# First chunk's replicas on TensorE instead of through DRAM, and later constants off VectorE, in a selective-scan kernel

## The chip, the cores and the metric

The kernel runs on one core of a Trainium2 chip, in one launch. The metric is the device time of an execution in microseconds, the median of three runs. Everything is float32. The core has five engines with a queue each: TensorE (PE, with its weight loads PEld), VectorE (DVE), ScalarE (ACT), GpSimd (POOL) and SyncE (SP), which issues nearly all DMAs here. Every engine works through its own instructions in the order in which the program emits them.

## The reference

The input x is 4 x 128 x 128 x 128. Layer 0 is a selective state-space layer along the 16,384 positions of each image; layer 1 is a Fourier-domain filter. The change lies almost wholly in layer 0, whose core is:

```python
u = silu(conv1d(x_in) + conv_b)                 # 256 channels
dt, Bm, Cm = split(u @ x_proj_w.T)              # 8, 16, 16
delta = softplus(dt @ dt_proj_w.T + dt_proj_b)
A = -exp(A_log)                                 # 256 x 16
h = h * exp(delta * A) + delta * Bm * u         # per position, state 256 x 16
y = sum(h * Cm) + u * D
```

After it come a gate with silu(z), an output projection, a group norm, silu and a residual. Layer 1 takes a group norm, a 1x1 product with `agg_w`, a pooled softmax over four filters, and a filter applied in the frequency domain.

## The kernel before

Layer 0 is cut into 128 chunks of 512 positions (32 chunks for each of 4 images). The 256 channels are two halves `j`; a half is 4 groups of 32 channels (`DG`). The 16 states are 4 sets of 4 (`SQ`). A work item for a scan is a 128x512 tile: 32 channels times 4 states on the partitions, 512 positions along the free dimension. A chunk has 8 **units**, (j, r), of 4 such tiles each, p = 0 to 3, and 16 **slots** (`NP`): a slot handles two tiles of a unit. Slots are the clock of a hand-written order: every step of the program has a slot number and a phase within the slot, all steps are sorted by these, and instructions are emitted in that order. Steps that prepare chunk k (`pre(k)`) start up to 14 slots ahead of their own chunk's count.

For a tile four things are needed:

- `da` = exp(delta * A): ScalarE, line L409, from `rdelta`, a copy of 32 channels' delta on 4 x 32 partitions (a *replica*).
- the input term. For p = 0 it comes as `b`, from TensorE: du = delta * u is transposed (`du_turn`, L306), scaled by each of 4 states' B and written as `bt` (`bt_act`, L318, 16 instructions a chunk on ScalarE), and transposed back (`dbu_turn`, L399). For p = 1 to 3 GpSimd multiplies `rdu`, the replica of du, with `rB` (`dbu`, L379) into `hb`.
- the scan itself, on VectorE (L428), four 128x512 scans a unit.
- the product with `rC`: on VectorE for p = 2, 3 (L430) and on GpSimd for p = 0, 1 (L435); TensorE then sums over states into `y` (L449). ScalarE keeps the last state of every scan (L431 and L575).

Ahead of that, chunk k goes through `load`, `h1` (L207, L212), `xm` (L217, L225), the convolution as 8 products (L242), silu (L247), `xd` (L258, L262), dt (L281), delta by Softplus (L287), and z (L231, L236, its Silu at L250). `xd` holds B and C as well: it is written to DRAM (`bc`, L266) and read back by `bc_load` (L274) with every row spread over 32 partitions. The replicas go the same way: delta and du are written to DRAM (`dd`, L289 and L325) and read back by `rep_load` (L333), four DMAs of 256 KB for each of delta and du and each half j. du itself is a GpSimd product (`du_pool`, L324). ScalarE reloads its function table (1.28 us each) when it changes between Exp, Silu and Softplus.

For chunk 0 nothing runs ahead of it to cover this preparation. There `rep_load` and `bc_load` are issued in an order of their own on SP: replica of delta, B, replica of du, C. TensorE does chunk 1's `h1` and `xm` between the two `du_turn` of chunk 0.

`first_constants` loads the weights and prepares some of them on VectorE (`wck`, L102; `amat`, L104 and L105; `diag`, L108). `later_constants` loads what later stages need, and `later_products` (L136 to L146), emitted after the scans of slot 33 (chunk 2), prepares these on VectorE: `fwm` negated, `eps`, `ones`, `weff0` from two products, and `bias0` from a TensorE product.

PSUM tiles come from small pools: `pp` (two banks), `pt`, `y`, and one bank each for `b0`, `da1`, `da2`, `da3`; a tile waits until the bank's former reader is done. Layer 1 follows after the last chunk and is not touched.

## Time and profile before

| | |
|---|---|
| median of 3 runs | 7065.94 us (7059.47 to 7074.77) |
| profiled execution | 7065.28 us |
| its span | 7063.4 us |
| VectorE busy | 6838.7 us (97%) |
| GpSimd busy | 6806.9 us (96%) |
| ScalarE busy | 6167.3 us (87%) |
| TensorE busy | 5631.0 us (80%) |
| granted TensorE clock, mean | 0.93 |

Times in the profile count from the start of the span. A timeline line gives start, duration, engine, source line, operation, out <- in, shapes, the number of instructions merged (x), and in brackets how long the engine was idle before and what ended that. A waits line gives who waited for whom, total us, times, longest. Names without numbers stand for all chunks' tiles; PEq and SPq are the sequencers of TensorE and SyncE.

### The profile page before, as it was taken

The page shows a single profiled execution, that of the slowest core. Times are in us where ns is not written, and L with a number is a line of the kernel's source. Part 1 is how long each engine was busy: PE and PEld are TensorE (multiplying, and loading weights), DVE is VectorE, ACT ScalarE, POOL GpSimd, SP SyncE. Part 2 cuts the span into 40 slices and gives each one's busy share as a digit, 9 for nine tenths or more (in the row PEclk, how much of TensorE's full clock was granted, in tenths as well). Part 3 has the DMA queues.
Part 4 walks back from the last instruction along what each step waited for, and adds up shares of the span by engine and source line. Part 5 has one row for each costly group of instructions (what it writes and reads, how often), then busy time and mean ns, then how long its engine had stood idle before and what let it go on. Part 6 is the DMA issues. An engine that isn't in the chain of part 4 may idle for free. (4 is left out here: it accounts for less than half of the span.)

```text
span 7063.4 us, 95476 instructions
## 1 busy us (share of the span) xinstructions
PE 5631.0 (80%) x28724; PEld 2681.6 (38%) x28724; DVE 6838.7 (97%) x7901; ACT 6167.3 (87%) x13836; POOL 6806.9 (96%) x3010
## 2 busy tenths in 40 slices
PE   7777777777777778887777788888777787878999
PEld 3333333333333333333333333333333333337888
DVE  7999999999999999999999999999999999998877
ACT  7888888888989888889999988889999988888886
POOL 7999999999999999999999999999999999997887
PEclk8899999999989989999999999999999999989999
DMA  6766766666778777777878777777877877777865
GB/s 152 164 161 150 164 158 153 161 156 165 194 183 194 182 168 174 179 179 171 201 190 196 196 170 175 178 179 170 201 191 192 200 173 175 173 174 273 272 221 192
DMA packets 759512, 1288.53 MB, mean 182 GB/s; under 512 B 81728, under 2 KB 192848, under 8 KB 758992
## 3 DMA queue, kind: packets, MB, share of 16 engines
q1 hardware_dynamic: 758704, 1281.90, 73.1%
q8 instruction: 226, 3.70, 0.2%
q14 instruction: 294, 2.41, 0.1%
q10 hardware_dynamic: 288, 0.52, 0.0%
HBM read 1025.52 MB, written 256.58 MB: 182 GB/s over the span
## 5 line engine op out<-in xcount | busy, mean ns | idle before, releaser
L379 POOL TENSOR_TENSOR hb<-rdu,rB 128x1536 f32<-128x1536 f32 (+2 forms) x1536 | 3613.1, 2370 | 38.5 <-DMA rdu<-dd 25.4
L409 ACT ACTIVATE da<-rdelta,amat 128x512 f32<-128x512 f32 x4096 | 2805.3, 704 | 105.6 <-DVE h L428 100.4
L435 POOL TENSOR_TENSOR hb<-h,rC 128x1024 f32<-128x1024 f32 (+1 forms) x1048 | 2410.3, 2301 | 75.1 <-DVE h L428 62.5
L428 DVE TENSOR_TENSOR_SCAN da<-da,st,hb 128x512 f32<-128x512 f32 x2000 | 2445.9, 1265 | 34.8 <-ACT da L409 34.1
L430 DVE TENSOR_TENSOR hb<-da,rC 128x512 f32<-128x512 f32 x2064 | 1307.8, 672 | 2.2
L428 DVE TENSOR_TENSOR_SCAN h<-da,st,b 128x512 f32<-128x512 f32 x992 | 1256.5, 1267 | 4.3 <-PE b L399 4.3
L449 PE MATMUL y<-hb,sel 128*32 128x512 f32 x8192 | 1242.8, 680 | 14.8 <-POOL hb L435 13.9
L428 DVE TENSOR_TENSOR_SCAN h<-da,st,hb 128x512 f32<-128x512 f32 x976 | 1221.5, 1253 | 2.6 <-ACT da L409 1.5
L399 PE MATMUL b<-ident,bt 128*128 128x128 f32 x4096 | 714.1, 295 | 492.9 <-DVE h L428 427.1
L242 PE MATMUL pp_cv<-xm,wck 128*128 128x512 f32 x2048 | 989.3, 627 | 2.9 <-ACT zs L236 1.6
L318 ACT ACTIVATE bt<-pt_dut,xdt 128x256 f32<-128x256 f32 x2048 | 851.0, 484 | 138.4 <-PE pt_dut L306 137.8
L399 PEld LDWEIGHTS b<-ident,bt 128*128 128x128 f32 x4096 | 517.1, 149 | 951.8 <-DVE h L428 704.3
L431 ACT COPY st<-da 128x1 f32<-128x1 f32 x2064 | 287.5, 163 | 446.1 <-DVE hb L430 442.3
L242 PEld LDWEIGHTS pp_cv<-xm,wck 128*128 128x128 f32 x2048 | 387.0, 199 | 633.5 <-issue 453.1
L306 PE MATMUL pt_dut<-ident,du 128*128 128x128 f32 x1024 | 198.3, 327 | 482.4 <-POOL du L324 451.5
L871 POOL TENSOR_TENSOR wb<-wb,term 128x1040 f32<-128x1040 f32 x166 | 398.9, 2403 | 50.2 <-ACT term L861 44.4
L445 PE MATMUL y<-u,diag 128*128 128x512 f32 x512 | 313.7, 697 | 163.5 <-DVE zs L459 163.0
L306 PEld LDWEIGHTS pt_dut<-ident,du 128*128 128x128 f32 x1024 | 140.8, 164 | 660.4 <-POOL du L324 590.5
L409 ACT ACT_TABLE_LOAD x262 | 336.1, 1283 | 4.6
L324 POOL TENSOR_TENSOR du<-delta,u 128x1024 f32<-128x1024 f32 x128 | 301.4, 2354 | 24.9 <-ACT delta L287 24.9
L449 PEld LDWEIGHTS y<-hb,sel 128*32 128x32 f32 x8192 | 170.4, 113 | 384.2 <-issue 244.5
L281 PE MATMUL pp_dt<-xd,wdt 128*128 128x256 f32 x1024 | 286.6, 404 | 25.9 <-ACT xd L262 8.9
(167 smaller groups left out, 8337.5 us busy)
## 6 DMA issues: line engine op xcount, KB each, us to landing
rdelta<-dd SPq DMA_DIRECT2D x1024, 256.0 KB, 4.9
rdu<-dd SPq DMA_DIRECT2D x1024, 256.0 KB, 7.8
rC<-bc SPq DMA_DIRECT2D x512, 256.0 KB, 7.1
rB<-bc SPq DMA_DIRECT2D x512, 192.0 KB, 4.4
dd<-delta SPq DMA_DIRECT2D x256, 256.0 KB, 7.6
dd<-du SPq DMA_DIRECT2D x128, 512.0 KB, 6.7
ft<-in_filt_w SPq DMA_DIRECT2D x108, 520.0 KB, 6.5
xr<-in_x SPq DMA_DIRECT2D x128, 256.0 KB, 3.0
```

The lines of the kernel that those rows point to most:

```text
L242: nc.tensor.matmul(ps["cv", j], w, d["xm"][:, t : t + T], start=t == 0, stop=t == KC - 1)
L306: nc.tensor.transpose(ps["dut"][:, 2 * t + j, :], d["du"][:, j, at : at + P], s.ident)
L318: nc.scalar.activation(d["bt"][:, 2 * h + t, :, q, :], src, AF.Copy, scale=d["xdt"][:, 2 * h + t, R + q : R + q + 1])
L379: nc.gpsimd.tensor_tensor(hb[:, p : p + n, :], d["du", j][:, m : m + n, :], d["B"][:, p - 1 : p - 1 + n, :], ALU.mult)
L399: nc.tensor.transpose(b[:, t * P : (t + 1) * P], src, s.ident)
L409: nc.scalar.activation(da, d["delta", j][:, m, :], AF.Exp, scale=s.amat[:, c : c + 1])
L428: nc.vector.tensor_tensor_scan(o, das[q], b, init, ALU.mult, ALU.add)
L430: nc.vector.tensor_tensor(hb[:, p + q, :], das[q], d["C"][:, p + q, :], ALU.mult)
L435: nc.gpsimd.tensor_tensor(hb[:, ps, :], h[:, q, :], d["C"][:, ps, :], ALU.mult)
L445: nc.tensor.matmul(y, s.diag[:, j, :], d["u"][:, j, :], start=True, stop=False)
L449: nc.tensor.matmul(y[m * DG : (m + 1) * DG, :], s.sel, d["hb", j, r][:, p, :], start=False, stop=r == NG - 1)
L871: nc.gpsimd.tensor_tensor(wb, wb, u[n].terms[f], ALU.add)
```

## The change

All of it concerns the preparation of chunk 0, that of chunk 1, and the constants.

- **Replicas of chunk 0, half j = 0.** `rep_mm` multiplies delta (or du) by `rep`, a 128 x 4 x 128 matrix made of copies of the identity's columns, so that TensorE writes 32 channels onto 4 x 32 partitions of a PSUM bank; `rep_copy` moves each of 8 such banks to SBUF, two on VectorE and six on ScalarE. The first half of chunk 0 no longer goes through `dd`; the second half does as before.
- **du of chunk 0** is made on VectorE in two products (`first_du`).
- **The 16 scaled pieces `bt` of chunk 0** are shared: ScalarE makes the 8 of du's first half of positions, VectorE the 8 of the second, from two PSUM banks (`pt` and `y`).
- **B and C of chunk 0** are loaded first on SP, ahead of the `dd` writes and the replicas.
- **Function tables**: a 1-element activation (`table`) of Softplus, and later of Exp, is put ahead of the first use.
- **Chunk 1's preparation**: load, `h1` and `xm` move ahead in the order (into banks `da1` to `da3`), most other steps move one slot back.
- **GpSimd's first product** of chunk 0 is split in one of 512 and one of 1024 columns.
- **Constants**: `eps` and `ones` are set at the start; `amat` is computed after chunk 0's `h1`; `later_products` goes from slot 33 to slot 39 and does `bias0`, `fwm` and the first product of `weff0` on ScalarE, moves that product to PSUM with an identity product on TensorE, and adds the second on VectorE.

```diff
     def first_constants(s):
+        s.eps = cpool.tile([P, 1], F32, tag="eps", name="eps")
+        nc.vector.memset(s.eps, EPS)
+        s.ones = cpool.tile([P, P], F32, tag="ones", name="ones")
+        nc.vector.memset(s.ones, 1.0)
...
-        nc.scalar.activation(amat, amat, AF.Exp)
-        nc.vector.tensor_scalar_mul(amat, amat, -1.0)
+        rep = s.rep = s.spare.tile([P, ND, P], F32, tag="o", name="rep", bufs=3)
+        for m in range(SQ):
+            nc.vector.tensor_copy(rep[:, :, m * DG : (m + 1) * DG], s.ident.rearrange("p (g d) -> p g d", d=DG))
...
+    def decay_rates(s):
+        nc.scalar.activation(s.amat, s.amat, AF.Exp)
+        nc.vector.tensor_scalar_mul(s.amat, s.amat, -1.0)
...
     def later_products(s, psum):
-        nc.vector.tensor_scalar_mul(s.fwm, s.fwm, -1.0)
-        nc.vector.memset(s.eps, EPS)
-        nc.vector.memset(s.ones, 1.0)
-        weff0 = s.weff0 = cpool.tile([P, C], F32, tag="weff0", name="weff0")
-        nc.vector.tensor_scalar_mul(weff0, s.wagg[:, 0, :], s.gam[:, 0:1])
-        nc.vector.scalar_tensor_tensor(weff0, s.wagg[:, 1, :], s.gam[:, 1:2], weff0, ALU.mult, ALU.add)
...
-        nc.vector.tensor_add(s.bias0, pb0[:, 0:1], s.bagg)
+        nc.scalar.activation(s.bias0, pb0[:, 0:1], AF.Identity, bias=s.bagg)
+        nc.scalar.mul(s.fwm, s.fwm, -1.0)
+        weff0 = s.weff0 = cpool.tile([P, C], F32, tag="weff0", name="weff0")
+        nc.scalar.activation(weff0, s.wagg[:, 1, :], AF.Copy, scale=s.gam[:, 1:2])
+        pw0 = psum("weff0")
+        nc.tensor.matmul(pw0[:, 0:C], s.ident, weff0, start=True, stop=True)
+        nc.vector.scalar_tensor_tensor(weff0, s.wagg[:, 0, :], s.gam[:, 0:1], pw0[:, 0:C], ALU.mult, ALU.add)
...
             def bt_act(h, n0, n1):
...
+                    if k == 0 and h:
+                        nc.vector.tensor_scalar_mul(o, src, scale)
+                    else:
+                        nc.scalar.activation(o, src, AF.Copy, scale=scale)
...
+            def first_du():
+                du = d["du"] = pq.tile([P, NH, T], F32, tag="du", name=f"du_{k}")
+                for j in range(NH):
+                    nc.vector.tensor_mul(du[:, j, :], d["delta"][:, j, :], d["u"][:, j, :])
+                nc.sync.dma_start(out=d["dd"][1, P:, :], in_=du[:, 1, :])
+            def table(f):
+                t = tiny.tile([P, 1], F32, tag="table", name=f"table_{f}")
+                nc.scalar.activation(t, s.ones[:, 0:1], f)
+            def rep_mm(tag, m, to):
+                ps[tag, m] = to(f"rep_{tag}_{m}")
+                nc.tensor.matmul(ps[tag, m], s.rep[:, m, :], d[tag][:, 0, :], start=True, stop=True)
+            def rep_copy(tag, m, copy):
+                if (tag, 0) not in d:
+                    d[tag, 0] = p2.tile([P, ND, T], F32, tag=f"r{tag}", name=f"r{tag}_{k}_0")
+                copy(d[tag, 0][:, m, :], ps[tag, m])
...
+            if k == 0:
+                return [
+                    (-14, "pe", load), (-7, "pe", h1_mm), (-6, "act", h1_act), (-5, "pe", xm_mm), (-4, "act", xm_act),
+                    (0, "pe", partial(cv_mm, 0)), (1, "pe", partial(cv_mm, 1)), (2, "act", silu_act),
+                    (3, "pe", xd_mm), (4, "act", xd_act), (4, "act", partial(table, AF.Softplus)), (5, "pe", dt_mm),
+                    (5, "pe", xd_turn), (5, "act", bc_load), (6, "act", dt_act), (6, "act", xd_turn_act),
+                    (6, "act", partial(table, AF.Exp)), (6, "dve", first_du),
+                    (7, "pe", partial(du_turn, 1)), (7, "pe", partial(du_turn, 0)),
+                    (8, "pe", partial(rep_mm, "delta", 0, psum)), (8, "pe", partial(rep_mm, "delta", 1, psum)),
+                    (8, "pe", partial(rep_mm, "du", 1, partial(bank, "da2"))),
+                    (8, "pe", partial(rep_mm, "du", 2, partial(bank, "da3"))),
+                    (8, "act", partial(bt_act, 0, 0, 8)), (8, "dve", partial(bt_act, 1, 0, 8)),
+                    (8, "dve", partial(rep_copy, "delta", 0, dve)), (8, "dve", partial(rep_copy, "delta", 1, dve)),
+                    (14, "act", partial(rep_copy, "du", 1, act)), (14, "act", partial(rep_copy, "du", 2, act)),
+                    (15, "pe", partial(rep_mm, "du", 3, psum)), (15, "act", partial(rep_copy, "du", 3, act)),
+                    (15, "pe", partial(rep_mm, "delta", 2, psum)), (15, "act", partial(rep_copy, "delta", 2, act)),
+                    (15, "pe", partial(rep_mm, "delta", 3, turn_bank)), (15, "act", partial(rep_copy, "delta", 3, act)),
+                    (15, "pe", partial(rep_mm, "du", 0, y_bank)), (16, "act", partial(rep_copy, "du", 0, act)),
+                    (10, "pe", partial(rep_load, 1)),
+                    (NP, "pe", z_mm), (NP, "act", z_act), (NP + 3, "act", z_silu),
+                ]
+            late = k == 1
...
+                (-14 - 10 * late, "pe", load), (-7 - 13 * late, "pe", h1_mm), (-6 - 13 * late, "act", h1_act),
+                (-5 - 6 * late, "pe", xm_mm), (-4 - 6 * late, "act", xm_act),
+                (late, "pe", partial(cv_mm, 0)), (1, "pe", partial(cv_mm, 1)), (2 + late, "act", silu_act),
...
-                n = min(NG - p, ND - m)
+                n = min(NG - p, ND - m) if u or p > 1 else 1
...
+        todo[-NP - 5, "act"].insert(0, partial(s.decay_rates, s))
-        todo[2 * NP + 1, "end"].append(partial(s.later_products, s, psum))
+        todo[2 * NP + 7, "end"].append(partial(s.later_products, s, psum))
...
-            todo[n - 1, "exps"].append(partial(exps, n, (1,) if n % 2 == 0 else (0, 1)))
+            todo[n - 1 - (n == 0), "exps"].append(partial(exps, n, (1,) if n % 2 == 0 else (0, 1)))
...
-                todo[n - 2, "dbu"].append(partial(dbu, n // 2))
+                todo[n - 2 + (n == 0), "dbu"].append(partial(dbu, n // 2))
```

## The prediction

> **What bounds the kernel now.** I first read the windows (busy time of each engine by stage, first numbers: length, then PE, PEld, DVE, ACT, POOL).
>
> ```profile
> 20.00:40.00 20.00, 11.92 (x39) 5.58 (x37) 0.00 (x0) 13.35 (x29) 2.34 (x1) 0.88 0.61 156
> 40.00:60.00 20.00, 15.20 (x43) 5.88 (x43) 12.51 (x13) 11.60 (x20) 14.76 (x6) 0.78 1.07 221
> 80.00:100.00 20.00, 17.35 (x76) 6.93 (x75) 20.00 (x22) 16.77 (x42) 20.00 (x9) 1.00 0.78 162
> 140.00:180.00 40.00, 31.60 (x120) 13.49 (x121) 39.41 (x43) 29.17 (x62) 35.43 (x15) 0.79 0.58 134
> ```
>
> From about 50 us on VectorE and GpSimd are both full, and VectorE stays so (499.8 of 500 us in the window 500 to 1000). So a microsecond at the start, or of VectorE work later, goes to the end almost whole, if GpSimd can follow. Only the first 50 us and one spot near 150 us are open to this change. Second, the waits of the first 100 us:
>
> ```profile
> DVE h L428 <- PE b L399: 30.1, 1, 30.1
> POOL hb L379 <- DMA rdu<-dd: 17.6, 1, 17.6
> DVE h L428 <- POOL hb L379: 6.9, 1, 6.9
> ```
>
> VectorE waits for the transposed pieces `b`, then for GpSimd's first product, which waits for the DRAM replica of du. Third, the timeline of the start, which dates these events, and VectorE's near 150 us:
>
> ```profile
> 24.70 0.92 SPq L289 DMA_DIRECT2D dd<-delta  x2
> 25.33 2.34 POOL L324 TENSOR_TENSOR du<-delta,u 128x1024 f32<-128x1024 f32 x1 [24.89 <-ACT delta L287]
> 28.48 1.94 ACT L318 ACTIVATE bt<-pt_dut,xdt 128x256 f32<-128x256 f32 x5 [3.04 <-PE pt_dut L306]
> 38.34 1.73 SPq L333 DMA_DIRECT2D rdu<-dd  x4
> 45.24 6.82 POOL L379 TENSOR_TENSOR hb<-rdu,rB 128x1536 f32<-128x1536 f32 x2 [17.57 <-DMA rdu<-dd]
> 48.71 1.22 DVE L428 TENSOR_TENSOR_SCAN h<-da,hb 128x512 f32<-128x512 f32 x1 [6.86 <-POOL hb L379]
> 53.26 1.21 DVE L428 TENSOR_TENSOR_SCAN h<-da,b 128x512 f32<-128x512 f32 x1
> ...
> 149.92 4.22 DVE L136 TENSOR_SCALAR fwm<-fwm 128x130 f32<-128x130 f32 x1
> 155.29 0.16 DVE L146 TENSOR_TENSOR bias<-pp_bias,agg_b 128x1 f32<-128x1 f32 x1 [0.55 <-PE pp_bias L145]
> 155.37 1.27 DVE L428 TENSOR_TENSOR_SCAN h<-da,st,b 128x512 f32<-128x512 f32 x1
> ```
>
> My marks are: VectorE begins unit 1 at 53.26, GpSimd ends its first two units at 52.06 (45.24 + 6.82), and the constants hold VectorE from 149.92 to 155.37, 5.45 us.
>
> **The change part by part.** Times are from the span's start; each is worked out from before's rows.
>
> *Front end.* TensorE now runs chunk 1's two h1 products before chunk 0's convolution. Their input is issued on SP at 8.86 (its place in SP's queue is unchanged) and the fastest landing of such a tile is 2.6 us, so 11.5; four passes at 0.45 us end at 13.2. The convolution began at 12.45, so +0.75 us; what queues behind the wait is the convolution and all of chunk 0. Moving `amat`'s Exp behind the Relus saves nothing here: xm is ready at about 10.5 and waits for the load. Then as before: 7.1 us of convolution, silu, xd, so xd ends at 22.2 (before 21.44).
>
> *Tables.* The Softplus table (1.28 us) was loaded at 22.69, when the dt product was ready. The 1-element dummy puts it beside that product: 22.2 to 23.5, dummy 0.25, delta 23.75 to 25.05 (two of 0.64). Before it ended at 25.26. The Exp table load moves too, from 37.32 to 25.35, with no change of count on ScalarE's path: table and dummy 1.55, xm of chunk 1 0.9, so ScalarE is free at 27.8.
>
> *du on VectorE.* GpSimd took 2.34 us (25.33 to 27.67). Two 128x512 products at 0.66 (rows L430 0.67, L459 0.66) overlap the second delta: end 25.8. Both transposes of du (0.66 each) end at 27.15 without waiting for a bank.
>
> *Scaled pieces.* ScalarE's 16 were spread to 40.06 by the second transpose and chunk 1's steps. Now ScalarE does 8 at 0.39 (5 in 1.94): 27.8 to 30.9. VectorE's 8 from PSUM are in no row: nearest are 0.28 (TENSOR_SCALAR 128x128) and 0.42 (COPY 128x256 from PSUM), far end 0.66 (128x512 product). I take 0.40, the same size: 26.5 to 29.7; at 0.66 it would end at 31.8 and cost about 2.
>
> *Replicas.* TensorE copies: eight 128x512 products, two passes each, 0.9 at 0.45 a pass (0.43 to 0.45 in the convolution), 1.77 at the slow 0.885 seen from 28.22. At 0.9 the first four end at 30.75. VectorE evicts delta 0 and 1 at 0.65 (between 0.55 for 128x384 and 0.66): 30.35 and 31.0. ScalarE: two Exp (0.69) to 32.3, du 1, 2, 3 at 0.535 (`zs`: two in 1.07) to 32.85, 33.4, 33.9, delta 2 and 3 to 35.0, three Exp to 37.05, du 0 to 37.6. Gone from SP's queue ahead of `rC`: eight replica issues of 256 KB, and half of each `dd` write; `rB` is issued at about 24.2, lands by 31.2 (7.0 us, the median there), `rC` by about 36: neither ends a wait, but were they late by more than 1.7 and 2.5 us they would.
>
> *First units.* GpSimd: 1.26 from 32.9, 2.35 to 36.5, then 3.43 from 37.65: 41.1, against 52.06: 10.9 earlier. VectorE: the third scan starts at 36.5 and unit 1 3.41 later (49.85 to 53.26 before): 39.9, 13.3 earlier. GpSimd no longer has a lead: 41.1 against the scan that needs it at 41.1; before 52.06 against 54.39.
>
> *What is late next.* ScalarE, in order. Silu's and Exp's table loads (2.57), z's Silu (1.06) and u's (1.25) now lie later relative to the scans, because chunk 1's steps are one slot later and the last-state copies before them wait for VectorE's products. I count unit 2's third scan waiting 1.8 us for its Exp, and unit 4's 0.6 behind Softplus. VectorE's 13.3 becomes 10.9, the same as GpSimd's. Bounds: nothing lost (13.3), or twice that (8.5).
>
> *Later constants.* Six VectorE instructions and a wait, 5.45 us, leave. One stays: 0.35, from PSUM. It waits for the last-state copy 0.16, bias 0.3, fwm and weff0 on ScalarE at 0.42 (row L676, 128x128), TensorE 0.35: 1.65 after the last product. That is 2.0 in place of 5.45, a saving of 3.4; VectorE's whole queue is behind it. If ScalarE and TensorE are ahead, 5.1; if ScalarE is late by the width of Exp pairs, 1.3 less. GpSimd can take the gain: it waited 3.85 us at 157.89 for just this. The 4.22 ends with GpSimd's instructions (150.47 + 3.57 = 154.04), while a TENSOR_SCALAR of the same width next to no GpSimd work took 0.16 at 154.20. eps and ones move to VectorE's idle start (0.23 us, idle until 7.95); the rep copies (four at about 0.2) and diag end at 10.6, before xm is needed at 13.2. Chunk 2 onward has the same instruction order on every engine except here.
>
> [...]
>
> [...] In the trace, TensorE's granted clock was 0.50 in 41 to 45 us after an idle of 2.40, and a pass took 0.89. After an idle of 1.82 (9.69) a pass took 0.50. [...]
>
> **Sum.** 10.9 + 3.4 = 14.3. The profiled execution took 7065.28 (span 7063.4 and 1.9 around it), 0.7 below the median 7065.94. 7065.3 - 14.3 = **7051 us**.
>
> **The rivals.**
> 1. *More gets through.* ScalarE is not late and the weff0 wait is hidden: 13.3 + 5.1 = 18.4, 7047. For it: my two waits assume that every copy in ScalarE's queue waits to the end; before's same place cost only 0.25 and 0.27. Against: GpSimd's own lead of 10.9.
> 2. *The start feeds late.* The replicas run at half clock (3.5 more), or VectorE's pieces at 0.66 (2), or the xt of chunk 1 lands after 8.2 us, the slowest seen (5.6). One or two of these: gain 6 to 10, 7055 to 7059. For it: the slow passes at 28.22; against: TensorE is busier than then.
> 3. *The start is hidden.* Something else than VectorE and GpSimd paces chunks 1 and 2 (chunk 1's softplus, `dd` write and replicas are one slot later), and only the constants count: 3.4, 7062. Against: no wait of VectorE on DMA in that range; before had 17 us from du's end (74.1) to its use (91.51), after the same.
> 4. *Slower.* Tiles moved in SBUF (eps, ones, the dummy) or a shifted phase of ScalarE against VectorE make each later chunk dearer. It needs 14.3 us over some 126 chunks to eat the gain, and 28.4, 0.23 us a chunk, to be slower by 0.2%. ScalarE's Exp waits at chunk turns are the place. At 0.28 a chunk: 7086. Against: same order; VectorE idles under 0.2 us in 500. From 2500 to 3000 it idles 8.7, so there is something to disturb.
>
> **How the numbers follow.** 0.2%, what a measurement tells from no change here, is 14.1 us: below 7051.8 is faster, over 7080.1 slower. Forecast 0.48 (7048 to 7055), rival 1 0.22, rival 2 0.17, rival 3 0.05, rival 4 0.08. Of the forecast I put 0.34 on the faster side, as both its waits are counted at their worst. Faster 0.34 + 0.22 = 0.56, slower 0.08, same 0.36. The range leaves rival 4 and half of rival 3 above: to 7063. Below, rival 1 with the median's own scatter (runs differ by 6 to 9): 7040.
>
> **What would show it.** First GpSimd product at 32 to 34 us; VectorE's scans without a long gap from about 36; unit 1 at 39 to 41; a wait of VectorE on ScalarE's Exp of 1 to 2 us near 48; delta's end near 25; convolution start near 13.2; replica products at 0.9; no 4 us instruction on VectorE near 137 to 145, and under 2 us of wait for pp_weff. I am wrong if xt lands late, if GpSimd starts after 37, or if later windows of 500 us take more than before.

## The result, and the profile after

The changed kernel took 7042.62 us (median of 9 runs, 7031.45 to 7049.56) beside 7065.94 for the kernel before (9 runs, 7049.93 to 7074.77): a ratio of 0.997, 95% interval 0.9961 to 0.9979. The profiled execution of the changed kernel took 7042.62 us, its span was 7040.8. Together with the runs beside the experiments, the kernel before has a mean of 7061.7 us (62 runs) and the changed one of 7042.9 (20 runs): 18.7 us less, give or take 3.0 (twice the standard error; single runs scatter by 6).

First the windows of the changed kernel, at the four stretches that were shown of before (length, then PE, PEld, DVE, ACT, POOL):

```profile
20.00:40.00 20.00, 18.52 (x65) 9.53 (x65) 12.08 (x19) 17.93 (x38) 6.63 (x3) 1.00 0.67 159
40.00:60.00 20.00, 13.89 (x70) 6.48 (x68) 18.41 (x20) 16.88 (x29) 20.00 (x10) 0.95 0.74 161
80.00:100.00 20.00, 18.45 (x82) 7.98 (x83) 20.00 (x22) 15.71 (x32) 20.00 (x9) 1.00 0.72 144
140.00:180.00 40.00, 29.18 (x129) 12.47 (x127) 37.35 (x40) 34.73 (x78) 39.32 (x18) 0.87 0.55 133
```

From 20 to 40 us VectorE does 12.1 us of work where it did none; GpSimd is full from 40 us on, where it had 14.8 of 20. Near 150 us VectorE has lost some of its fill (37.4 of 40) while GpSimd has gained (39.3, was 35.4): the 3.85 us that GpSimd waited there are gone.

Second, the timeline of the changed kernel, start and later constants (start, duration, engine, line, operation; L488 and L490 are the scans and VectorE's products, L439 and L495 GpSimd's products, L360 the copies of the replicas):

```profile
26.80 3.22 DVE L334 TENSOR_SCALAR bt<-dut,xdt 128x256 f32<-128x256 f32 x8 [1.04 <-ACT tivationFunctionType.Exp L351]
26.96 1.88 PE L355 MATMUL pp_rep_delta<-delta,rep 128*128 128x512 f32 x4
27.30 3.01 ACT L336 ACTIVATE bt<-dut,xdt 128x256 f32<-128x256 f32 x8
30.65 1.30 ACT L469 ACTIVATE da<-rdelta,amat 128x512 f32<-128x512 f32 x2 [0.34 <-DVE rdelta L360]
32.55 3.58 POOL L439 TENSOR_TENSOR hb<-rdu,rB 128x512 f32<-128x512 f32 x2 [32.10 <-ACT rdu L360]
36.16 2.35 DVE L488 TENSOR_TENSOR_SCAN da<-da,hb 128x512 f32<-128x512 f32 x2 [1.08 <-POOL hb L439]
36.94 3.45 POOL L439 TENSOR_TENSOR hb<-rdu,rB 128x1536 f32<-128x1536 f32 x1 [0.82 <-ACT rdu L360]
39.59 1.21 DVE L488 TENSOR_TENSOR_SCAN h<-da,b 128x512 f32<-128x512 f32 x1
49.16 2.35 DVE L488 TENSOR_TENSOR_SCAN da<-da,hb 128x512 f32<-128x512 f32 x2 [1.59 <-POOL hb L495]
61.18 2.35 DVE L488 TENSOR_TENSOR_SCAN da<-da,hb 128x512 f32<-128x512 f32 x2 [0.60 <-ACT da L469]
...
157.83 0.33 ACT L148 ACTIVATE fwm<-fwm 128x130 f32<-128x130 f32 x1
158.03 0.41 ACT L150 ACTIVATE weff<-wagg,gn_gamma 128x128 f32<-128x128 f32 x1
158.50 0.80 PE L152 MATMUL pp_weff<-weff,ident 128*128 128x128 f32 x2 [3.66 <-ACT weff L150]
159.33 0.35 DVE L153 SCALAR_TENSOR_TENSOR weff<-wagg,gn_gamma,pp_weff 128x128 f32<-128x128 f32 x1 [2.65 <-PE pp_weff L152]
```

The trip through DRAM is gone: GpSimd starts at 32.55 instead of 45.24, VectorE begins unit 1 at 39.59 instead of 53.26. Two waits of VectorE are new (1.59 at unit 2, where before had 0.25 and 0.27, and 0.60 at unit 4), and the constants cost it 2.65 of waiting and 0.35 of work.

For a measure that no late scatter touches I take, in each trace, the start of the first scan of every unit of layer 0 (1024 units; unit 0 opens chunk 0, eight to a chunk). How much earlier a unit starts in the changed kernel is its **lead**. From unit 1 on it is 13.67 us, 11.6 at unit 13, 17.1 at unit 17 (only before has done its constants), 14.06 at unit 20, 14.0 to 14.8 through unit 500 (some 3100 us), and then 25.8 at unit 1023. From there to the end, layer 1 included, the changed kernel gives back 3.2 (708.6 us against 705.4), which leaves the 22.6 between the two spans. So two things need an explanation: which part makes the 14, and where the 11 after unit 650 come from.

### The profile page after: what moved, and what is told of

Its sections match the earlier page's. It is cut to its first block, busy times and chain, and to the rows that moved or that the text cites. A ratio compares the mean times of both kernels' runs of the same rounds, so it can differ in the third digit from the quotient of the medians.

```text
span 7040.8 us, 95517 instructions
## 1 busy us (share of the span) xinstructions
PE 5615.9 (80%) x28742; PEld 2685.4 (38%) x28742; DVE 6840.5 (97%) x7914; ACT 6167.2 (88%) x13839; POOL 6802.5 (97%) x3010
## 5 line engine op out<-in xcount | busy, mean ns | idle before, releaser
L439 POOL TENSOR_TENSOR hb<-rdu,rB 128x512 f32<-128x512 f32 (+2 forms) x1537 | 3614.3, 2370 | 62.4 <-ACT rdu L360 32.9
L488 DVE TENSOR_TENSOR_SCAN da<-da,st,hb 128x512 f32<-128x512 f32 x2000 | 2446.9, 1266 | 25.3 <-ACT da L469 24.7
L495 POOL TENSOR_TENSOR hb<-h,rC 128x1024 f32<-128x1024 f32 (+1 forms) x1048 | 2411.9, 2303 | 55.0 <-DVE h L488 45.0
L490 DVE TENSOR_TENSOR hb<-da,rC 128x512 f32<-128x512 f32 x2064 | 1308.8, 673 | 2.2
L488 DVE TENSOR_TENSOR_SCAN h<-da,st,b 128x512 f32<-128x512 f32 x992 | 1257.6, 1268 | 2.7 <-PE b L459 2.7
L509 PE MATMUL y<-hb,sel 128*32 128x512 f32 x8192 | 1233.6, 675 | 12.9 <-POOL hb L495 12.5
L488 DVE TENSOR_TENSOR_SCAN h<-da,st,hb 128x512 f32<-128x512 f32 x976 | 1222.6, 1255 | 2.8 <-POOL hb L495 2.1
L336 ACT ACTIVATE bt<-dut,xdt 128x256 f32<-128x256 f32 x2040 | 845.3, 483 | 114.7 <-PE dut L320 113.6
L320 PE MATMUL dut<-ident,du 128*128 128x128 f32 x1024 | 199.0, 328 | 475.4 <-POOL du L340 450.3
L505 PE MATMUL y<-u,diag 128*128 128x512 f32 x512 | 307.1, 684 | 166.2 <-DVE zs L519 165.4
L320 PEld LDWEIGHTS dut<-ident,du 128*128 128x128 f32 x1024 | 141.9, 165 | 651.6 <-POOL du L340 582.0
L244 PE MATMUL pp_z<-xm,win 128*128 128x512 f32 x512 | 274.8, 634 | 39.0 <-ACT fq L577 37.0
```

What stands on the lines that cost most here:

```text
L320: nc.tensor.transpose(ps["dut", h][:, 2 * t + j, :], d["du"][:, j, at : at + P], s.ident)
L336: nc.scalar.activation(o, src, AF.Copy, scale=scale)
L439: nc.gpsimd.tensor_tensor(hb[:, p : p + n, :], d["du", j][:, m : m + n, :], d["B"][:, p - 1 : p - 1 + n, :], ALU.mult)
L488: nc.vector.tensor_tensor_scan(o, das[q], b, init, ALU.mult, ALU.add)
L490: nc.vector.tensor_tensor(hb[:, p + q, :], das[q], d["C"][:, p + q, :], ALU.mult)
L495: nc.gpsimd.tensor_tensor(hb[:, ps, :], h[:, q, :], d["C"][:, ps, :], ALU.mult)
```

## The experiments

Theory A: the 14 us are the sum of the early steps, and the later 11 are scatter that has nothing to do with the change. Theory B: the change shifts something that makes later chunks cheaper. Within the start, theory A holds that one chain (delta, du, its transposes, the pieces, the first Exp, ScalarE's copies, GpSimd) sets everything; rival R that replicas and GpSimd do so alone. Starts of units are given below from the start of the first convolution product, `cv`, for a reason that the control shows.

**Start alone.** The changed kernel, with the body of `later_products` as in the kernel before (`fwm`, `weff0` and `bias0` on VectorE) and in its old slot.

```diff
-        nc.scalar.mul(s.fwm, s.fwm, -1.0)
+        nc.vector.tensor_scalar_mul(s.fwm, s.fwm, -1.0)
...
-        todo[2 * NP + 7, "end"].append(partial(s.later_products, s, psum))
+        todo[2 * NP + 1, "end"].append(partial(s.later_products, s, psum))
```

> The new start with the later constants prepared as before (on VectorE, at their old place). Theory A (the early gain is what the change made, the further gain in the second half of the first layer is scatter of TensorE's clock between executions): VectorE's lead over the kernel before, taken at the first scan of a unit, is 13.5 to 13.8 us at unit 1, 11.6 at unit 13, and stays 11 to 12.5 through unit 300, since the 5.45 us of the constants are paid again; the time is about 12 us less than before, 0.998, give or take the scatter. Theory B (the further gain of some 8 us comes with the new start, by a shift of phase): the lead is again some 12 until unit 650 and then grows to 20 or more at unit 1023, and the ratio is near 0.997.

Measured: 7044.4 us, ratio 0.9977 (0.9967 to 0.9987). Lead 13.9 at unit 1, 11.86 at 13, 12.07 at 20 and 12.08 at 300; 24.5 at unit 1023. The early half of theory A holds to 0.5 us. The late growth is as B has it, but see the control.

**Constants alone.** The kernel before, with the body of `later_products` as changed, in its new slot, and `eps` and `ones` set at the start.

```diff
-        nc.vector.tensor_scalar_mul(s.fwm, s.fwm, -1.0)
+        nc.scalar.mul(s.fwm, s.fwm, -1.0)
...
-        todo[2 * NP + 1, "end"].append(partial(s.later_products, s, psum))
+        todo[2 * NP + 7, "end"].append(partial(s.later_products, s, psum))
```

> The old start with the later constants prepared by ScalarE and TensorE, two chunk slots later than before. Theory A: the lead is 0 until unit 16 and then 5.45 - (2.65 wait + 0.35 sum) = 2.4 us, staying between 2 and 3.5 through unit 300; the time is 2 to 4 us less than before, ratio 0.9995, not to be told from 1. Theory B with the later gain tied to the constants' place: the lead grows by 5 us or more after unit 650 and the ratio is 0.9985 or less.

Measured: 7060.44 us, 0.9992 (0.9983 to 1.0001). The lead is -1.27 from unit 1 to 13 and 1.20 at unit 20: a gain of 2.46, the same as in the changed kernel between units 13 and 20 (14.06 - 11.61 = 2.45). The -1.27 are not of the constants. The lead grows to 14.1 by the end here too.

**Both kernels once more**, nothing edited.

> The changed kernel once more, nothing edited. Theory A: the lead at units 20 to 300 is again 14.0 to 14.5 us, to 0.3 us; from unit 650 to 1023 it grows by anything between -8 and +10 us, not by the same +11.7 as in the first profile, and the turns of chunks whose seventh unit lasts 7.2 instead of 5.9 us are other ones. Theory B: the growth is within 3 us of the first profile's 11.7, at the same chunks.

> The kernel before once more, nothing edited: ratio 1.000 within its interval, whose half width (about 0.001) is what a comparison can tell. Theory A: against the first profile of the same kernel its lead is 0 within 0.3 us until unit 300 and drifts by several us (5 to 12, either sign) by unit 1023, at turns of chunks where VectorE waits 1.3 us for ScalarE's Exp. Theory B: it stays within 2 us of the first profile to the end.

Measured: the changed kernel 7044.01 us, 0.9978 (0.997 to 0.9987), its lead 14.63 at unit 20, 14.84 at 300 and 18.2 at 1023: it grows by 3.4 where the first profile grew by 11.4. The kernel before took 7059.65, 0.9994 (0.9985 to 1.0002), with a lead on its own first profile of -1.8 until unit 400 and +8.3 at unit 1023. An unedited kernel thus gains 10 us on itself between units 400 and 1023: a late part of this size comes without any change, and the first profile of before was an unlucky one. The -1.8, which I had not expected, has a row. The second product of the start, in the timeline of the kernel before and of its second execution:

```profile
9.69 1.98 PE L217 MATMUL pp_xm<-h,w 128*128 128x512 f32 x4 [1.82 <-ACT h L212]
12.45 4.13 PE L242 MATMUL pp_cv<-xm,wck 128*128 128x512 f32 x9 [0.78 <-ACT xm L225]
```

```profile
9.86 3.65 PE L217 MATMUL pp_xm<-h,w 128*128 128x512 f32 x4 [2.00 <-ACT h L212]
14.28 1.98 PE L242 MATMUL pp_cv<-xm,wck 128*128 128x512 f32 x4 [0.78 <-ACT xm L225]
```

Four passes of `xm` took 1.98 us in the one and 3.65 in the other (3.67 in the constants-alone run), so the convolution began at 12.45, 14.28 and 13.67 in three executions of that front end, and at 13.38, 12.85 and 13.16 in three of the changed one, where it waits for chunk 1's tile instead. Counted from the convolution the traces agree within 0.1 us:

| unit's first scan, from cv | unit 1 | unit 13 | unit 20 |
|---|---|---|---|
| kernel before | 40.81 | 112.32 | 161.21 |
| kernel before, again | 40.84 | 112.37 | 161.13 |
| changed | 26.21 | 99.78 | 146.22 |
| changed, again | 26.22 | 99.74 | 146.18 |
| start alone | 26.21 | 99.75 | 148.43 |

That is 15.0 us at unit 20: 12.5 from the start (unit 13) and 2.4 from the constants.

**Four undoings of the start**, each in the changed kernel: no dummy activations; the first half's replicas through DRAM; all 16 pieces on ScalarE; du on GpSimd.

```diff
-                    (3, "pe", xd_mm), (4, "act", xd_act), (4, "act", partial(table, AF.Softplus)), (5, "pe", dt_mm),
+                    (3, "pe", xd_mm), (4, "act", xd_act), (5, "pe", dt_mm),
...
-                    (6, "act", partial(table, AF.Exp)), (6, "dve", first_du),
+                    (6, "dve", first_du),
```

```diff
-                    (8, "pe", partial(rep_mm, "delta", 0, psum)), (8, "pe", partial(rep_mm, "delta", 1, psum)),
...
-                    (15, "pe", partial(rep_mm, "du", 0, y_bank)), (16, "act", partial(rep_copy, "du", 0, act)),
+                    (8, "pe", partial(rep_load, 0)),
...
-                for j in range(k == 0, NH):
+                for j in range(NH):
...
-                nc.sync.dma_start(out=d["dd"][1, P:, :], in_=du[:, 1, :])
+                nc.sync.dma_start(out=d["dd"][1].rearrange("(j p) t -> p j t", p=P), in_=du)
```

```diff
-                    if k == 0 and h:
+                    if False:
                         nc.vector.tensor_scalar_mul(o, src, scale)
```

```diff
-                    nc.vector.tensor_mul(du[:, j, :], d["delta"][:, j, :], d["u"][:, j, :])
+                    nc.gpsimd.tensor_tensor(du[:, j, :], d["delta"][:, j, :], d["u"][:, j, :], ALU.mult)
```

> The changed kernel without the two small activations that call up the tables of Softplus and Exp ahead of their use. Times are from the start of the first convolution product, where the changed kernel has its second unit's first scan at 26.21 us in both profiles and its unit 20 at 146.2. Theory A (the second unit is reached by the chain delta, du, its turning, the scaled pieces, ScalarE's first Exp, ScalarE's copies, GpSimd): the Exp table's load of 1.28 us comes behind the eight scaled pieces and only 0.34 us of it is hidden, so the second unit comes at 27.15; Softplus changes nothing, because its load goes ahead while ScalarE waits. Rival R (the replicas and GpSimd set the second unit by themselves, and ScalarE has room): 26.2 to 26.4.

> The changed kernel, but the first half's replicas of delta and du go through DRAM again, as in the kernel before, with the constants, the pieces shared with VectorE and du on VectorE left as changed. Theory A (the replicas on TensorE carry most of the start's gain): the trip of 17.6 us from du to GpSimd's first product stands again, from du's end at 12.4 us after the first convolution product: GpSimd starts at about 30 and the second unit comes at 38 (35 to 40) where the changed kernel has 26.2 and the kernel before 40.8; so the replicas are worth some 12 us and the rest of the start 3. Rival R (the earlier pieces and scans carry it, the trip being hidden behind GpSimd's other waits): 32 or less.

> The changed kernel with all 16 scaled pieces of the first chunk on ScalarE. Theory A: ScalarE's second eight pieces take 3.0 us more ahead of its first Exp, so the first scan comes at 20.7 to 21.0 instead of 18.0 from the first convolution product and the second unit at 28.9 to 29.2 instead of 26.21. Rival R (the replicas set the second unit): the first scan moves, the second unit stays within 1 us of 26.2.

> The changed kernel with du on GpSimd, in the same two halves. Theory A: GpSimd takes 1.2 to 1.8 us for a half where VectorE takes 0.69, so du ends 1.2 to 2.2 us later, the turning, the pieces and the first Exp with it, and the second unit comes at 27.4 to 28.4 instead of 26.21. Rival R (the pieces are hidden behind the replicas of delta): within 0.6 us of 26.2.

| from cv | first scan | unit 1 | GpSimd ends units 0 and 1 | unit 13 | unit 13 less GpSimd's end | time, one run |
|---|---|---|---|---|---|---|
| kernel before | 28.18 | 40.81 | 39.61 | 112.32 | 72.71 | - |
| changed | 18.03 | 26.21 | 27.01 | 99.78 | 72.77 | - |
| no dummy activations | 19.68 | 27.88 | 28.66 | 101.44 | 72.78 | 7038.25 |
| replicas by DRAM | 29.79 | 40.77 | 40.70 | 113.43 | 72.73 | 7052.95 |
| pieces on ScalarE | 20.51 | 28.71 | 29.50 | 102.31 | 72.81 | 7039.22 |
| du on GpSimd | 18.85 | 27.05 | 27.84 | 100.56 | 72.72 | 7041.92 |

(GpSimd's end is the end of its third group of products, `hb<-rdu` for units 0 and 1; for the kernel before 52.06 - 12.45. The single times were taken beside 7064.46 for the kernel before and differ by less than such runs scatter; the marks do not.)

Each undoing moves unit 1 by its own amount, so the chain is one (rival R, which allowed 0.2, 1.0 and 0.6 us for the first, third and fourth, falls with 1.67, 2.50 and 0.84). The sizes that I had given missed in all four, the third by little:

- *Dummy activations*: 1.67 us, not 0.94. The rows of that kernel show why Softplus counts:

```profile
23.51 1.28 ACT L300 ACT_TABLE_LOAD   x1 [1.25 <-PE pp_dt L294]
24.80 1.27 ACT L300 ACTIVATE delta<-pp_dt,dt_b 128x512 f32<-128x512 f32 x2
...
31.00 1.28 ACT L469 ACT_TABLE_LOAD   x1
32.30 1.30 ACT L469 ACTIVATE da<-rdelta,amat 128x512 f32<-128x512 f32 x2
```

  ScalarE idles 1.25 us for the dt product and loads the table only then, so delta and du come 1.1 us later; 0.67 of that reaches the pieces, and the rest, 1.0, comes with Exp's load behind them.
- *Replicas by DRAM*: 40.77, not 38. The trip from du's end to GpSimd's first product took 21.4 us and not the 17.6 that I had carried over: the product is at 47.38 from the span's start, 33.7 from cv, against 32.8 in the kernel before, although du ends 2.8 us earlier (both from cv). B and C are still loaded first here, so the first write of delta landed 7.8 us after its issue (2.0 in the kernel before), and the loads of du's replicas stand right behind those of delta's. So with this order on SP the rest of the start brings 0.04 us at unit 1 and loses 1.1 at unit 13: without the replicas on TensorE nothing of the gain is left. How much of the 14.6 us at unit 1 the replicas are worth alone this run does not separate; with a trip of 17.6, unit 1 would stand at about 37 (an estimate, 40.77 less 3.8), which would leave them some 11.
- *Pieces on ScalarE*: 2.50, a little under the 2.7 to 3.0 expected (16 pieces took 5.95 us, 8 took 3.01).
- *du on GpSimd*: 0.84, where 1.2 to 2.2 was expected. GpSimd took 2.48 us for the halves, VectorE 1.37; in the changed kernel TensorE is busy with chunk 1's xm product until 0.3 us after du's end, so that much of the delay cost nothing (in this run TensorE waited 0.61 for du).

The last but one column is what I had not foreseen. Wherever the start ends, unit 13 comes 72.7 to 72.8 us after GpSimd's end of units 0 and 1. In the trace of the changed kernel GpSimd has no pause at all from 36.94 to 174.5 us, in that of before none from 45.24 to 154.0, where it begins to wait for the constants. In this stretch GpSimd is the pace, and VectorE's waits are where its surplus lead (13.67 at unit 1 against 11.6) goes. The place where the two meet is in the changed kernel's rows:

```profile
111.15 1.11 PE L320 MATMUL dut<-ident,du 128*128 128x128 f32 x4 [6.94 <-POOL du L340]
113.16 1.28 DVE L488 TENSOR_TENSOR_SCAN h<-da,st,b 128x512 f32<-128x512 f32 x1 [0.64 <-PE b L459]
```

GpSimd makes du of chunk 2 from 108.77 to 111.10. TensorE's transposes of it wait for that, unit 13's `b` (112.06) stands behind them in TensorE's order, and VectorE waits 0.64 us for `b`. In eleven of the thirteen traces unit 13 starts 2.06 us after the end of this product; the other two (2.08 with the replicas by DRAM, 2.29 in the last kernel below) are those in which VectorE does not wait there.

**Silu apart.** The wait of 1.59 us at unit 2 stands in the profile against GpSimd; its neighbour on ScalarE is one visit to the Silu table of 4.8 us. The first chunk's Silu of the gate moves two slots on.

```diff
-                    (NP, "pe", z_mm), (NP, "act", z_act), (NP + 3, "act", z_silu),
+                    (NP, "pe", z_mm), (NP, "act", z_act), (NP + 5, "act", z_silu),
```

> The changed kernel with the first chunk's Silu on the gate taken two slots later, so that ScalarE's visit to the Silu table is two visits of 3.6 to 3.8 us, with two Exps between, in place of one of 4.9. Theory A (the 1.59 us that VectorE loses ahead of unit 2's third scan, which the profile puts down to GpSimd, is the wait for ScalarE's Exp behind that visit): the wait falls to 0.3 to 0.7, unit 3 comes at 38.1 to 38.4 us from the first convolution product instead of 39.2, and unit 20 about 1 us earlier than 146.2. Rival (GpSimd's product is what is late, as the profile names it): unit 3 stays at 39.2.

The waits of VectorE in this kernel's timeline:

```profile
47.93 2.35 DVE L488 TENSOR_TENSOR_SCAN da<-da,hb 128x512 f32<-128x512 f32 x2 [0.66 <-issue]
54.64 2.35 DVE L488 TENSOR_TENSOR_SCAN da<-da,hb 128x512 f32<-128x512 f32 x2 [0.95 <-ACT da L469]
61.37 2.35 DVE L488 TENSOR_TENSOR_SCAN da<-da,hb 128x512 f32<-128x512 f32 x2 [0.96 <-ACT da L469]
```

The wait falls to 0.66 and unit 3 comes at 38.29 (39.22 without the edit), so it was ScalarE's Exp, not the product that the profile names. Yet unit 5 comes at 51.73 (51.24), unit 13 at 99.76, unit 20 at 146.20, the last two as without the edit. My "1 us earlier at unit 20" fails. The edit did not take a wait away but moved it: the second visit to the Silu table stands in front of other Exps, and VectorE loses 0.95 at unit 3 and 0.96 at unit 4 instead, 2.57 us in the three waits where it lost 2.19. So this run does not show what a removed wait is worth. Unit 13 stays all the same, its wait for `b` falling from 0.64 to 0.31, as GpSimd is no earlier than it was. The single run took 7048.13.

**The closing sum one slot later.** VectorE's last addition of `weff0` goes behind the next unit's first two scans.

```diff
-        nc.vector.scalar_tensor_tensor(weff0, s.wagg[:, 0, :], s.gam[:, 0:1], pw0[:, 0:C], ALU.mult, ALU.add)
+        return lambda: nc.vector.scalar_tensor_tensor(
+            weff0, s.wagg[:, 0, :], s.gam[:, 0:1], pw0[:, 0:C], ALU.mult, ALU.add
+        )
...
-        todo[2 * NP + 7, "end"].append(partial(s.later_products, s, psum))
+        add = []
+        todo[2 * NP + 7, "end"].append(lambda: add.append(s.later_products(s, psum)))
+        todo[2 * NP + 8, "dve"].append(lambda: add[0]())
```

> The changed kernel with VectorE's closing sum of the combined weight given out one slot later, behind the next pair of scans. Theory A (VectorE loses 2.65 us there only because it stands in front of TensorE's result): the wait is under 0.2 us and unit 20 comes at 143.5 us from the first convolution product instead of 146.2. Rival: the wait covers something that is late anyway (ScalarE's Exp behind its three extra activations), which then stands at the next scan: unit 20 at 145 or later.

The wait is 0.29 us (under 0.2 expected) in place of 2.65, unit 20 comes at 143.17 (expected 143.5), and 2.4 of the 3.0 us are still there at unit 50 (327.02 against 329.40), so the rival falls. GpSimd has no pause there either (none until 174.5 in the changed kernel), and yet this wait of VectorE counted. One run took 7040.92.

**GpSimd first.** To test the pace of GpSimd directly, its operands come sooner: ScalarE's copies of du's replicas go ahead of the Exps of their pair (the closing sum as in the last one).

```diff
-                    (14, "act", partial(rep_copy, "du", 1, act)), (14, "act", partial(rep_copy, "du", 2, act)),
+                    (13, "act", partial(rep_copy, "du", 1, act)), (13, "act", partial(rep_copy, "du", 2, act)),
...
-                    (15, "pe", partial(rep_mm, "du", 0, y_bank)), (16, "act", partial(rep_copy, "du", 0, act)),
+                    (15, "pe", partial(rep_mm, "du", 0, y_bank)), (15, "act", partial(rep_copy, "du", 0, act)),
...
-                todo[n - 3, "early"].append(partial(exps, n, (0,)))
+                todo[n - 3 + (n == 2), "early"].append(partial(exps, n, (0,)))
```

> The changed kernel with VectorE's closing sum one slot later, as in e3_sum_later, and with ScalarE's copies of du's replicas put ahead of the Exps of their pair, so that GpSimd gets its operands sooner. Times are from the start of the first convolution product. Theory A (from the first unit on GpSimd has no pause, so the moment at which it ends the products of units 0 and 1, 27.0 us in the changed kernel and 39.6 in the kernel before, sets where unit 13 stands, whatever VectorE's lead is in between): it ends them 1.5 to 1.9 us sooner, at 25.1 to 25.5, unit 1 moves by less than 0.5 us (25.9 to 26.2), unit 13 comes at 97.9 to 98.4 instead of 99.75, unit 20 at 141.4 to 141.9 (143.2 in e3_sum_later), and the time is 4 to 5 us under that of the changed kernel, about 0.9965 of the kernel before. Rival (ScalarE's visits to other tables set the pace of units 2 to 5, as its waits of 1.59 and 0.60 us say): GpSimd pauses instead, and unit 13 stays within 0.4 us of 99.75.

The timeline of this kernel:

```profile
30.59 1.27 POOL L441 TENSOR_TENSOR hb<-rdu,rB 128x512 f32<-128x512 f32 x1 [30.15 <-ACT rdu L362]
32.79 5.77 POOL L441 TENSOR_TENSOR hb<-rdu,rB 128x1024 f32<-128x1024 f32 x2 [0.93 <-ACT rdu L362]
```

GpSimd ends units 0 and 1 at 25.47 from cv (27.01 in the changed kernel), 1.5 us sooner; unit 1 moves by 0.4 to 25.80, and unit 13 by 1.3 to 98.47 (97.9 to 98.4 expected), 73.0 after GpSimd's end, with ScalarE's waits of 1.59 and 0.60 unchanged. At unit 13 VectorE no longer waits, so the last 0.3 are its own. Unit 20 is at 141.70, 4.5 us ahead of the changed kernel. The time was 7038.25 (7 runs, mean 7040.4), 0.997 (0.9959 to 0.9981) of the kernel before. It is the best of all kernels here by its marks; the 2.6 us between the means of it and of the changed kernel (7042.9) are no more than these runs can tell.

**Where the late scatter sits.** The thirteen traces show it. From unit 300 to 1023 I added up the seven steps from unit to unit within a chunk and the one across its turn. Each of the seven sums differs by 3.2 us or less from trace to trace. Those across the turn make nearly all of the rest: a turn lasts 5.9 us in most chunks and 7.1 or more (a long turn) in 9 to 22 of 90.

| trace | long turns | all turns, sum in us | unit 300 to 1023, us |
|---|---|---|---|
| kernel before, first / again | 22 / 10 | 569.2 / 558.3 | 4475.2 / 4465.2 |
| changed, first / again | 14 / 17 | 559.5 / 566.6 | 4463.8 / 4471.9 |
| start alone, constants alone | 11, 11 | 557.4, 556.3 | 4462.8, 4462.7 |
| seven others | 9 to 16 | 554.7 to 565.5 | 4460.0 to 4472.4 |

Means over kernels with the old start (14 long turns, three traces) and with the new (13, ten traces) do not differ by more than their scatter: 4467.7 and 4465.0 us. What makes a turn long is seen in chunk 84. First the kernel before, where it is long (windows: busy times, then granted clock, DMA share, GB/s; and the timeline):

```profile
4222.00:4225.00 3.00, 3.00 (x10) 0.70 (x10) 3.00 (x4) 2.57 (x8) 3.00 (x3) 0.50 1.07 216
4225.00:4228.00 3.00, 3.00 (x10) 1.46 (x9) 3.00 (x4) 0.46 (x2) 3.00 (x3) 0.72 1.06 214
```

```profile
4224.42 3.09 PE L217 MATMUL pp_xm<-h,w 128*128 128x512 f32 x4
4227.99 1.21 ACT L318 ACTIVATE bt<-pt_dut,xdt 128x256 f32<-128x256 f32 x3 [2.54 <-PE pt_dut L306]
4233.56 2.47 DVE L428 TENSOR_TENSOR_SCAN da<-da,st,hb 128x512 f32<-128x512 f32 x2 [1.26 <-ACT da L409]
```

Then the changed kernel, where the same turn is short:

```profile
4206.00:4209.00 3.00, 3.00 (x11) 0.25 (x10) 3.00 (x5) 2.61 (x8) 3.00 (x2) 0.58 1.05 218
4209.00:4212.00 3.00, 3.00 (x19) 2.00 (x16) 3.00 (x4) 1.93 (x5) 3.00 (x3) 1.00 1.06 212
```

```profile
4208.97 1.98 PE L230 MATMUL pp_xm<-h,w 128*128 128x512 f32 x4
4211.43 1.20 ACT L336 ACTIVATE bt<-dut,xdt 128x256 f32<-128x256 f32 x3 [1.02 <-PE dut L320]
```

TensorE's granted clock drops to 0.50 a little ahead of the turn in both, from 4219.86 to 4226.69 us in the kernel before and from 4205.09 to 4208.50 in the changed one. In the kernel before it stays there into the next chunk's xm product (3.09 us instead of 1.98), which pushes the transposes of du behind it, ScalarE's pieces behind those, and its Exp, for which VectorE then waits 1.26. Over the turns of chunks 82 to 126 for which all four passes are recorded (44 in each trace), in both first traces and the second of the changed kernel: 20 of the 29 long turns have an xm product of 2.96 us or more, and the other 9 are the same three chunks in all three (82, 97 and 114, which last 8.2 to 9.6 us); of 103 short turns 3 have one. Why those three are long in every trace, no run here shows.

## Why the prediction was right, and where it was not

The forecast was 7051 us (7040 to 7063), faster with 0.56; the median is 7042.6, faster, inside the range.

- **Front end.** Convolution at 13.2 expected, 13.38 found (then 12.85 and 13.16), waiting for chunk 1's tile as worked out. The step "+0.75 us" is wrong as a difference: the 12.45 of before was the early one of three, 12.45, 13.67 and 14.28, by its xm product. On the mean of these three the front end loses nothing.
- **Chain to GpSimd.** Delta 23.68 to 25.03 (23.75 to 25.05 said), du's end 25.76 (25.8), transposes 27.12 (27.15), first four replicas 30.56 (30.75), eight pieces on VectorE at 0.40 each (0.40), first GpSimd product 32.55 (32.9), unit 1 at 39.59 (39.9). A replica took 0.94 us, near the 0.9 assumed, not 1.77: the granted clock was 1.00 from 20 to 40 us, with TensorE busy for 18.52 of the 20. The outcome was right. The two rows that the prediction sets beside each other, a pass of 0.89 us after an idle of 2.40 and one of 0.50 after 1.82, do not give the reason: in the kernel before the clock went to 0.50 at 38.54 us, ahead of the end of that idle (40.12), and what the traces show to go with it is how busy TensorE was in the 3.41 us before, here for 1.49 (last section). The new order kept it busy.
- **What is late next.** Unit 2's third scan was to wait 1.8 and unit 4's 0.6; they waited 1.59 and 0.60, and the lead fell from 13.67 to 11.6, where 13.3 to 10.9 had been said. The size was right; the reason stands half. ScalarE does cause these waits, but moving the larger to other places changed nothing at unit 13, and making GpSimd 1.5 us earlier gave 1.3 with both in place. The loss of about 2 us is the distance between VectorE's lead and GpSimd's, which the prediction had beside it as "the same as GpSimd's" and took for an agreement. GpSimd's end was the term to carry into the sum.
- **Later constants.** This is the mis-sized term: 2.0 us in place of 5.45 was the forecast, and 3.0 came (2.65 of waiting and 0.35), so 2.45 saved and not 3.4. I had let `bias0` start after one small copy. In the trace ScalarE also stands before an Exp of 0.72 and a copy of 0.28 between the end of VectorE's products (156.68) and 157.67, and TensorE took 0.80 for the identity product where I had 0.35; its granted clock was 0.50 from 158 to 160 us. The text had priced it as "late by the width of Exp pairs, 1.3 less", so it was in the bounds.
- **The 4.22 us on VectorE** for `fwm` were 4.20 again in the run with the start alone, and 0.33 on ScalarE. GpSimd was busy beside both, from 150.47 to 154.04 us in the kernel before and from 156.31 to 158.64 in the changed one. Why VectorE's took so long, no run here shows.
- **The sum.** 14.3 us against a lead of 14.06 at unit 20 in the two profiles, 15.0 when both are counted from the convolution. That the sum comes so close is luck in part: the start gave 11.6 where 10.9 was added and the constants 2.45 where 3.4 was, and the two errors cancel. The median fell by 23.3 in the first comparison and by 18.2 in the second; all runs give 18.7 (15.7 to 21.7). What lies above 15 in the first comparison is of the kind of scatter that the turns show, and the profile of before, with 22 long turns, was on the high side of it. Whether 3 us of it belong to the change is open: no trace shows a place for them.
- **The rivals.** 1 (more gets through) gave a time nearer to the measured one, but not by its mechanism: its two waits were there. The last kernel shows what it needs, a lead of 18.9 with the closing sum moved and GpSimd first. 2 fails with the replicas at 0.94 us, the pieces at 0.40 and chunk 1's tile landing after 2.65 us; its "8.2 us, the slowest seen" is that of the first 100 us, and later tiles of the kernel before took up to 10.4. 3 fails with the start's 12.5. 4 named the right place, ScalarE's Exp at the turns, but the later chunks are not dearer: 13 long turns in the mean against 14.

## What to carry to other kernels

When two engines are both almost full, look for the place where one has to wait for the other, and take the lead of a faster start from the engine that has no pause ahead of that place (here GpSimd, up to unit 13) and not from the other's visible waits: making GpSimd's first products end 1.5 us earlier gave 1.3, with VectorE's waits in place. This holds from unit 1 to 13 here; near unit 20 a wait of VectorE counted although GpSimd had no pause either. A result that another engine must hand back should be consumed one step later than it is asked for; here that is worth 2.4 us for a line moved. And for changes of 0.2%, compare marks inside the traces, from a common event, before comparing medians: they agreed to 0.1 us where runs differ by 20 and more.

## What the runs showed of the hardware

TensorE's half clock falls on the same work in one execution and not in the next. In chunk 84 the windows show a granted clock of 0.50 and 0.72 at the turn, around the next chunk's product, in one trace (4222 to 4228 us) and of 1.00 in the other (4209 to 4212), which costs VectorE 1.26 us two engines further on.

The traces show what goes with it (busy by the profile's rows, which model the ends of matmuls). In all thirteen the granted clock is 1.00 or 0.50 and holds for whole steps of 3.41 us (of the 187 stretches at half clock in the first trace of before, 89 last one step and 91 two). Of the steps at full clock, TensorE was busy for 55% or less of each of the 2267 that half clock followed (49% or less of 99 in 100), and for 41% or more of each of the 20,954 that full clock followed (48% or more of 99 in 100). Of the steps at half clock, it was busy for 83% or more of each of the 2254 after which the clock rose, and for 94% or less of each of the 1316 after which it did not. So in these traces a fall goes with a step that is busy for less than about half, and a rise with one that is almost full. The longest single pause inside a step tells the two apart less well: in the first traces of the two kernels it was 0.96 us or more in the 361 steps that half clock followed, and up to 2.01 in the 3200 that full clock followed. In chunk 84 the step ahead of the fall had 1.12 us of work in the kernel before and 0.85 in the changed one. The step after it began 0.69 and 0.42 us ahead of the same product (`y`, L445 and L505) and was busy for 2.72 and 2.99 us: in the one the clock stayed at half, in the other it rose.

The slow first xm products are another case. The four passes of h1 ahead of them, of the same shape, took 3.78 us in all three traces with the old front end; four such passes took 3.54 at a recorded clock of 0.50 (28.22 us, kernel before) and 1.98 at 1.00 (11.56 us, changed kernel). The trace's first record of a granted clock is one of full clock and stands at 7.82, 13.24 and 12.65 us. Of the xm products that begin at 9.69, 9.86 and 9.22 us, the first, which began behind that record, took 1.98 us; the others, which began ahead of it, took 3.65 and 3.67. The pause before them (1.82, 2.00 and 1.41 us) does not tell them apart.

A load of a ScalarE table, 1.28 us, did not go ahead of the wait of the instruction that needs it in the run without dummy activations (idle 1.25 us, then the load), while the Silu table at 14.29 us of the changed kernel was loaded before the wait of 1.45 for its operand. Why the two differ, no run here shows.
